# Zero fills of the edge matrix: eight small transfers for one, each tied to an earlier edge scatter

## The chip, the cores and the metric

The kernel runs on one core of a Trainium2 chip. The core has five engines, each with its own instruction queue: TensorE (PE), VectorE (DVE), ScalarE (ACT), GpSimd (POOL) and SyncE (SP), and sixteen DMA engines. The metric is the device time of one execution in microseconds (us). The time before is given as the median of five runs.

## What is computed

A network block of two layers over a graph with 3125 nodes and 50,000 edges (sorted by destination), 256 features. Each layer adds a graph convolution and an attention to the node features, and then a mixture of experts. Only the graph convolution of layer 0 matters here:

```python
def _L0_gnn_ref(input, edge_index, edge_weight, weight, bias):
    support = jnp.matmul(input, weight)
    row, col = (edge_index[0], edge_index[1])
    msgs = support[col] * edge_weight[:, None]
    output = jax.ops.segment_sum(msgs, row, num_segments=input.shape[0])
    return output + bias
...
xn = _layernorm(x, axis=-1)
x = x + _L0_gnn_ref(xn, edge_index, edge_weight, ...) + _L0_mix_ref(xn[None], ...)[0]
x = x + _L0_ffn_ref(_layernorm(x, axis=-1)[None], ...)[0]
```

## The kernel before

The convolution is done with a dense matrix of edge weights, `adj`, which lies in the chip's main memory (DRAM) and has 3200 x 3200 float32 elements. It goes through five steps.

1. *Zeros.* `adj` is cut into 25 pieces of 128 rows (`PIECE`, 1.6 MB). A DMA on SP's queue fills a piece from a tile of zeros (`fill`, L444 to L451, issued at L447). The tile has 128 x 800 elements and is read four times in one DMA, so the DMA has 512 rows of 3,200 bytes.
2. *Chunks.* The edges are cut into 16 chunks (`WIDTHS`: 8 and 12 columns, ten of 32, then 16, 16, 12 and 7; a column is 128 edges). SP loads a chunk's edges (`edge_load`, L372; the tiles of 32 columns have five buffers, so a load waits until DVE is done with the chunk five back). DVE works out the weights, with duplicate edges summed (`ch_code`, `ch_same`, `ch_prod`, `ch_sum`), and each edge's place in `adj` (`ch_place`, L415).
3. *Scatters.* POOL issues one indirect DMA per column (L75, `adj<-ch_sum,ch_place`, 391 in all), and behind each a small memset as a spacer (`spaced`, L286; the memset `idle`, L290). A chunk's scatters wait for the fills of all pieces that the chunk may touch ("zeros below").
4. *Row loads.* SP reads rows of `adj` back into SBUF (`load`, L541, two loads of 896 and 704 KB a piece), waiting for the scatters of the chunks that reach them.
5. *Runs.* PE multiplies them with the support (`sup`) in six runs of 4, 4, 4, 4, 4 and 3 pieces (`RUNS`, L572), DVE adds the results to `gT` (L578). Two last pieces come later.

Between these, PE, DVE and ACT sort the edges of the second layer in small steps (`sort_by_low`): DVE makes one-hot tiles (`s_hot`, L1350; `wi`, `we`, `wc`, L1353; `s_z`, L1361), ACT makes others (L1356, L1359), and PE multiplies them (L1377, L1382). `s_hot` has three buffers, so DVE waits for the matmul that read the one three steps back.

The order on PE, DVE, ACT and SP is the order of the program text. A generator `chunks()` is called on by estimated times (`advance`), and after each chunk's DVE work it puts that chunk's later edge load and some fills into SP's queue. Pieces that chunk c needs are numbered by `pieces_of(c)`: 1, 2, 4, 6, 8, ... 22, 23, 24, 25, 25. Before, the end of chunk c's work fills up to `pieces_of(c + 3)`; pieces 0 to 5 are filled by explicit calls ahead of it. Every hardware DMA, of SP and ACT alike, also carries one of eight semaphores and waits for the earlier DMA that had it.

Of the kernel before, what the change touches and what calls it, by code (L numbers as in the profile page):

```python
# [9 lines left out]
F32 = mybir.dt.float32  # L10
# [14 lines left out]
NP = NT * P  # L25
# [15 lines left out]
WIDTHS = (8, 12) + (32,) * 10 + (16, 16, 12, 7)  # L41
ENDS = [128 * sum(WIDTHS[:i]) for i in range(len(WIDTHS) + 1)]
EP, EW = 80, 625
PIECE = P * NP
# [5 lines left out]
PARTS = ((0, 4 * WIDE), (4 * WIDE, NP))  # L50
SW = 264
STEPS = 5
AHEAD = 90.0
RATE = 1.38

# [17 lines left out]
def scatter(nc, table, idx, rows, add=False):  # L73
    kw = {"compute_op": OP.add} if add else {}
    return nc.gpsimd.indirect_dma_start(  # L75
        out=table, out_offset=bass.IndirectOffsetOnAxis(ap=idx, axis=0),
        in_=rows, in_offset=None, **kw)


def pieces_of(c):  # L80

    return min(NT, (ENDS[c + 1] + DRIFT) // (16 * P) + 1)
# [35 lines left out]
def overlapping(ap, start, steps):  # L118

    return bass.AP(tensor=ap.tensor, offset=ap.offset + start,  # L120
                   ap=[list(ap.ap[0])] + [list(s) for s in steps])
# [6 lines left out]
class Kernel:  # L128
# [247 lines left out]
    def edge_chunk(self, pool, c):  # L376


        nc = self.nc
        e0 = ENDS[c]  # L380
        F, K = WIDTHS[c], HALO
        dst, src, W = self.chunk_in.pop(c)
        C = pool.tile([128, F + 2 * K], F32, name="ch_code", bufs=2)
        nc.vector.scalar_tensor_tensor(C, dst, float(NP), src, op0=OP.mult, op1=OP.add)
        same = pool.tile([128, F + K, K], BF16, name="ch_same", bufs=1)
        prod = pool.tile([128, F, K], F32, name="ch_prod", bufs=1)
        yield
        step = -(-F // 2) if F > 16 else F
        for f0 in range(-K, F, step):
            f1 = min(F, f0 + step)  # L390
            m = f1 - f0
            nc.vector.tensor_tensor(same[:, f0 + K:f1 + K, :], C[:, f0 + K:f1 + K, None].to_broadcast([128, m, K]),
                                    overlapping(C, f0 + K + 1, [[1, m], [1, K]]), OP.is_equal)
        yield
        for f0 in range(0, F, step):
            f1 = min(F, f0 + step)
            nc.vector.tensor_mul(prod[:, f0:f1, :], same[:, f0 + K:f1 + K, :],
                                 overlapping(W, f0 + 1, [[1, f1 - f0], [1, K]]))
        yield
        more = pool.tile([128, F], F32, name="ch_more", bufs=2)  # L400
        nc.vector.tensor_reduce(more, prod, AX.X, OP.add)
        wsum = pool.tile([128, F], F32, name=f"ch_sum{F}", bufs=4 if F == 32 else 2)
        nc.vector.tensor_add(wsum, more, W[:, :F])

        yield
        dup = pool.tile([128, F], F32, name="ch_dup", bufs=2)
        flat = same.rearrange("p i k -> p (i k)")
        nc.vector.tensor_reduce(dup, overlapping(flat, K - 1, [[K, F], [K - 1, K]]), AX.X, OP.max)
        own = C[:, K:K + F]
        off = pool.tile([128, F], F32, name="ch_off", bufs=2)  # L410
        nc.vector.scalar_tensor_tensor(off, self.number[F], float(BEHIND + e0), own,
                                       op0=OP.add, op1=OP.subtract)
        nc.vector.scalar_tensor_tensor(off, dup, self.off, off, op0=OP.max, op1=OP.mult)
        place = pool.tile([128, F], I32, name=f"ch_place{F}", bufs=4 if F == 32 else 2)
        nc.vector.tensor_add(place, off, own)  # L415
        ready = pieces_of(c)
        for f in range(F):
            ins = self.spaced(scatter(nc, self.adj[:], place[:, f:f + 1], wsum[:, f:f + 1]))
            for i in range(ready):
                self.after(ins, self.fills[i], "zeros below")  # L420
            self.tc.declare_no_dep(ins.ins, group="adj read", reason="blocks that are complete")
            for i in range(ready, NT):
                self.tc.declare_no_dep(ins.ins, group=f"zeros {i}", reason="rows behind the chunk's")
            for i in range(c + 1):
                self.tc.declare_no_dep(ins.ins, group=f"edges {i}", reason="places of their own")
            self.tc.add_to_no_dep_group(f"edges {c}", ins.ins)
            self.edge_scatters.setdefault(c, []).append(ins.ins)


    def layer0(self):  # L430
        nc, tc, a = self.nc, self.tc, self.a
        with ExitStack() as c:
# [5 lines left out]
            near = c.enter_context(ExitStack())  # L438
            ed = near.enter_context(tc.tile_pool(name="l0e", bufs=1))
            self.adj = self.dram.tile([BEHIND + 128 * NJ, 1], F32, name="adj")  # L440
            zero = ed.tile([128, NP // 4], F32, name="zero")
            nc.vector.memset(zero, 0.0)

            def fill(stop):  # L444
                for i in range(len(self.fills), stop):
                    rows = self.adj[i * PIECE:(i + 1) * PIECE].rearrange("(p r s) o -> p r (s o)", p=128, r=4)
                    ins = nc.sync.dma_start(rows, zero[:, None, :].to_broadcast([128, 4, NP // 4]))  # L447
                    for c in self.edge_scatters:
                        tc.declare_no_dep(ins.ins, group=f"edges {c}", reason="rows behind the chunk's")
                    tc.add_to_no_dep_group(f"zeros {i}", ins.ins)  # L450
                    self.fills.append(ins.ins.name)  # L451

            self.chunk_in, self.edge_scatters, self.fills, self.chunks_done = {}, {}, [], 0
            early = c.enter_context(ExitStack())
            big = early.enter_context(tc.tile_pool(name="l0x", bufs=1))
            order = self.edge_order(ed)
            next(order)
            self.edge_load(ed, 0, nc.sync)
            fill(1)
            for i in range(1, 3):  # L460
                self.edge_load(ed, i, nc.sync)
            self.load_x(nc.scalar)
            parts = [self.edges_by_tile(big), self.message_weights(big)]
            for g in parts:
                next(g)
            fill(4)
            for i in range(3, 7):
                self.edge_load(ed, i, nc.sync)
            fill(6)
            self.number = {}  # L470
            for F in sorted(set(WIDTHS)):
                self.number[F] = ed.tile([128, F], F32, name=f"number{F}")
# [2 lines left out]
            def chunks():  # L475
                for c in range(len(WIDTHS)):
                    steps = self.edge_chunk(ed, c)
                    for i in range(STEPS):
                        yield RATE * (ENDS[c] + (ENDS[c + 1] - ENDS[c]) * i / STEPS) / 128 - AHEAD
                        next(steps, None)  # L480
                    for _ in steps:
                        pass
                    self.chunks_done = c + 1
                    if c + 5 < len(WIDTHS) and c + 5 > 6:
                        self.edge_load(ed, c + 5, nc.sync)
                    fill(pieces_of(min(c + 3, len(WIDTHS) - 1)))
                yield 1e9

            prepared = chunks()
            due, now = next(prepared), 35.0  # L490

# [1964 lines left out]
```

## Time and profile before

| | |
|---|---|
| median of five runs | 3126.36 us (3106.69 to 3156.18) |
| profiled execution | 3102.36 us, span 3100.6 us |
| mean granted TensorE clock in it | 0.832 of full speed |
| PE busy | 2133.7 us (69%) |
| DVE busy | 1471.1 us (47%) |
| ACT busy | 823.6 us (27%) |
| POOL busy | 1699.5 us (55%) |
| fills of `adj` (L447) | 25, 1600 KB each |
| scatters into `adj` (L75) | 391, first at 22.1, last at 670.2 us |
| row loads of `adj` (L541) | 50, first at 335.6, last at 785.9 us |

All views of the profile come from one execution, taken by the hardware's profiler. "Busy" counts instructions at work and leaves out issues of DMAs; SP, which does nothing else, has no busy time. A wait is put down to the instruction whose semaphore came last ("releaser"); "issue" is time in which an engine waited for nothing that the profile shows, "remote" is a release that it can't assign. "PEld" is the loading of weights into TensorE and runs beside its matmuls. Lines (L75 and so on) are lines of the kernel before.

When the scatters of each chunk ran, in the profiled execution (us):

| chunk | start to end | chunk | start to end |
|---|---|---|---|
| 0 | 22.1 to 33.7 | 8 | 368.9 to 414.2 |
| 1 | 41.0 to 57.3 | 9 | 425.7 to 470.2 |
| 2 | 57.7 to 103.2 | 10 | 481.1 to 528.0 |
| 3 | 103.6 to 148.1 | 11 | 528.4 to 571.7 |
| 4 | 148.4 to 192.1 | 12 | 597.7 to 622.9 |
| 5 | 225.6 to 273.1 | 13 | 623.3 to 645.4 |
| 6 | 273.5 to 319.8 | 14 | 645.8 to 661.7 |
| 7 | 320.2 to 368.5 | 15 | 662.1 to 671.2 |

The matmuls of the six runs: 340.8 to 388.0, 387.8 to 448.3, 454.4 to 503.4, 590.7 to 643.2, 694.0 to 743.8 and 747.1 to 787.4 us. The fills left SP at 9.9 (piece 0), 34 to 40 (1 to 3), 52 to 86 (4 to 13), 210 (14, 15), 254 to 259 (16 to 19), 347 (20, 21), 390 (22) and 484 (23, 24); the row loads of runs 0 to 5 from 335.6, 367.9, 423, 484.8, 619 and 720 us.

### The profile page before, as it was taken

The numbers are of one execution on the slowest core, as the hardware profiler recorded it, in microseconds if no ns is written. First come the engines' busy times: TensorE is split into PE (matmuls) and PEld (weight loads), VectorE is DVE, ScalarE is ACT, GpSimd is POOL, SyncE is SP. The second block draws the span as 40 slices with busy tenths as digits, with TensorE's granted clock in tenths as the row PEclk, the third lists the DMA queues.
The fourth block names the chain that finished last, engine by engine and source line by source line (L and its number), as shares of the span: only waits on it lengthen the run. The fifth ranks groups of instructions, "written<-read, shape, count | busy, mean of one in ns | idle before, by whom it ended". The sixth has DMA issues, their size and how long they took to land.

```text
span 3100.6 us, 26794 instructions
## 1 busy us (share of the span) xinstructions
PE 2133.7 (69%) x8219; PEld 1479.8 (48%) x8219; DVE 1471.1 (47%) x3847; ACT 823.6 (27%) x1789; POOL 1699.5 (55%) x2187
## 2 busy tenths in 40 slices
PE   0555786569889998989984567676959222279944
PEld 0333353235455777777873344444646111146623
DVE  7348856565634941111114677777674000023345
ACT  0233143344422122222222233342014000012213
POOL 5858877550004446666630777778755888820011
PEclk9776797679859999999996798898978656689977
DMA  8312456022001245555533221222211001101122
GB/s 283 108 43 89 178 180 205 1 86 87 8 27 61 80 142 168 171 168 164 180 118 100 67 46 46 47 47 52 48 48 31 8 8 14 16 13 53 45 75 87
DMA packets 191718, 263.29 MB, mean 85 GB/s; under 512 B 57234, under 2 KB 152071, under 8 KB 191563
## 3 DMA queue, kind: packets, MB, share of 16 engines
q1 hardware_dynamic: 137551, 211.02, 20.6%
q0 software_dynamic: 48864, 45.64, 6.8%
q10 hardware_dynamic: 5148, 4.80, 0.5%
q8 instruction: 67, 1.10, 0.1%
q14 instruction: 88, 0.72, 0.1%
HBM read 180.80 MB, written 80.55 MB: 84 GB/s over the span
## 4 chain that ended last, share of the span: by engine, by line
PE 30%; issue 15%; DVE 11%; POOL 11%; another core or an unknown queue 9%; ACT 3%; DMA 2%; DVEq 0%; SPq 0%; POOLq 0%; ACTq 0%
POOL g L68 11%; PE pb L1137 6%; PE fpy L1867 5%; PE fph L1851 5%; PE pc L1146 4%; PE pb L572 3%; PE pb L615 1%; PE pc L1377 1%; DVE d_cum L1243 1%; PE pc L572 1%; PE fpy L2169 1%; DMA g<-tab,t_src 1%; DVE v L1623 1%; PE pb L273 1%
## 5 line engine op out<-in xcount | busy, mean ns | idle before, releaser
L68 POOL DMA_INDIRECT g<-tab,t_src x391 | 471.5, 1206 | 202.6 <-issue 199.3
L75 POOL DMA_INDIRECT adj<-ch_sum,ch_place x391 | 410.6, 1050 | 170.6 <-issue 63.8
L75 POOL DMA_INDIRECT sorted<-src,pos x256 | 245.2, 958 | 141.3 <-issue 77.9
L1851 PE MATMUL fph<-xT,fw 128*128 128x512 f32 (+2 forms) x448 | 193.4, 579 | 184.8 <-ACT fh L1853 172.0
L1137 PE MATMUL pb<-xs,w 128*128 128x256 f32 x1024 | 245.3, 395 | 44.8 <-ACT h L1139 41.5
L68 POOL DMA_INDIRECT G<-tabg,g_src x256 | 244.2, 954 | 42.7 <-issue 42.7
L1137 PEld LDWEIGHTS pb<-xs,w 128*128 128x128 f32 x1024 | 199.7, 197 | 85.3 <-ACT h L1139 49.9
L1629 PE MATMUL pw<-v,hot 128*128 128x260 f32 x782 | 231.1, 460 | 0.0
L1146 PE MATMUL pc<-w,h 128*128 128x256 f32 x1024 | 226.1, 379 | 0.0
L1851 PEld LDWEIGHTS fph<-xT,fw 128*128 128x128 f32 x448 | 89.8, 204 | 270.3 <-ACT fh L1853 178.1
L1867 PE MATMUL fpy<-fw,fh 128*128 128x256 f32 (+1 forms) x800 | 185.4, 390 | 34.5 <-issue 34.5
L572 PE MATMUL pb<-adj,sup 128*128 128x448 f32 (+1 forms) x484 | 199.1, 557 | 14.3 <-DVE r_tot L1248 13.6
L1146 PEld LDWEIGHTS pc<-w,h 128*128 128x128 f32 x1024 | 192.2, 190 | 24.9
L1139 ACT ACTIVATE h<-pb,b 128x256 f32<-128x256 f32 x256 | 115.8, 473 | 317.8 <-issue 248.3
L1853 ACT ACTIVATE fh<-fph,cols 128x512 f32<-128x512 f32 (+2 forms) x112 | 69.7, 632 | 487.7 <-remote 256.8
L1629 PEld LDWEIGHTS pw<-v,hot 128*128 128x128 f32 x782 | 177.0, 232 | 34.9
L1867 PEld LDWEIGHTS fpy<-fw,fh 128*128 128x128 f32 (+1 forms) x800 | 154.5, 194 | 70.3 <-issue 45.6
L68 POOL DMA_INDIRECT g_r<-sums,g_ati x25 | 24.5, 978 | 273.1 <-DMA sums<-g_joint 265.8
L1359 ACT ACTIVATE s_z<-s_y,s_val 128x128 f16<-128x128 f16 x256 | 112.4, 486 | 195.6 <-issue 190.7
L290 POOL MEMSET idle<- 128x128 f32 x697 | 154.2, 221 | 15.5 <-remote 12.5
L75 POOL DMA_INDIRECT slots<-rows,abi x50 | 58.1, 1163 | 164.6 <-DVE which L1060 154.9
L1869 DVE TENSOR_TENSOR acc<-fpy,fb 128x256 f32<-128x256 f32 (+1 forms) x25 | 10.6, 424 | 283.9 <-remote 217.3
(570 smaller groups left out, 3861.5 us busy)
## 6 DMA issues: line engine op xcount, KB each, us to landing
adj<-zero SPq DMA_DIRECT2D x25, 1600.0 KB
w<-in_L_ffn_W1p_dram SPq DMA_DIRECT2D x32, 1024.0 KB
w<-in_L_ffn_W2p_dram SPq DMA_DIRECT2D x32, 1024.0 KB
adj<-adj SPq DMA_DIRECT2D x24, 896.0 KB
adj<-adj SPq DMA_DIRECT2D x24, 704.0 KB
slots<-empty SPq DMA_DIRECT2D x1, 8448.0 KB
srow<-slots SPq DMA_DIRECT2D x32, 264.0 KB
adj<-ch_sum,ch_place POOLq DMA_INDIRECT x391
```

The costliest lines, as they stand in the source:

```text
L68: return nc.gpsimd.indirect_dma_start(out=out, out_offset=None, in_=table, in_offset=bass.IndirectOffsetOnAxis(ap=idx, axis=0))
L75: return nc.gpsimd.indirect_dma_start(out=table, out_offset=bass.IndirectOffsetOnAxis(ap=idx, axis=0), in_=rows, in_offset=None, **kw)
L290: rest = self.nc.gpsimd.memset(self.idle, 0.0)
L572: nc.tensor.matmul(pm[:, :w], sup[:, b, k * 128:(k + 1) * 128], mats[b, h][:, c0 - PARTS[h][0]:c0 - PARTS[h][0] + w], start=(b == b0), sto ...
L1137: nc.tensor.matmul(ph, w1[:, k, f * 128:(f + 1) * 128], xs[:, k, :], start=(k == 0), stop=(k == 1))
L1139: nc.scalar.activation(h[:, f, :], ph, AF.Gelu, bias=b1[:, f:f + 1])
L1146: nc.tensor.matmul(py, h[:, f, i * 128:(i + 1) * 128], w2[:, f, :], start=(f == 0), stop=(f == FC - 1))
L1359: nc.scalar.activation(z[:, i, k, :], y, AF.Relu, bias=val[:, k, s], scale=val[:, 2 + k, s])
L1629: nc.tensor.matmul(pw.rearrange("p h c -> p (h c)"), hot[:, k, :], v[:, k, :, :].rearrange("p h c -> p (h c)"), start=(k == 0), stop=(k == ...
L1851: nc.tensor.matmul(ph[:, :m], w1[:, k, f * 128:(f + 1) * 128], xT[:, k, t0 * P:t0 * P + m], start=(k == 0), stop=(k == 1))
L1853: nc.scalar.activation(hs[:, f, :m], ph[:, :m], AF.Gelu, bias=self.col("L1_ffn_b1", ei * FC + f))
L1867: nc.tensor.matmul(py[:p], hs[:, f, i * P:i * P + p], w2[:, f, :], start=(f == 0), stop=(f == FC - 1))
```

## The change

Each piece is filled by eight DMAs in place of one: the zero tile is 128 x 400 elements, and a small fill writes one of eight column blocks of the piece's 128 partition rows (128 rows of 1,600 bytes, 200 KB). There are 200 of them for 25. The early call for pieces 4 and 5 goes away; chunk 1's work issues them. The end of chunk c's work now fills up to `pieces_of(c + 2)` for `pieces_of(c + 3)`. And from chunk 2's on, the n-th small fill issued there waits for the spacer memset behind a scatter of chunk c - 2: the fills are spread evenly over that chunk's scatters (`edge_marks`). A scatter waits for all eight small fills of each piece below it. The order of instructions on PE, DVE, ACT and POOL stays as it was; SP has 175 more.

```diff
+SUBS = 8
...
             for i in range(ready):
-                self.after(ins, self.fills[i], "zeros below")
+                for name in self.fills[i]:
+                    self.after(ins, name, "zeros below")
...
             self.edge_scatters.setdefault(c, []).append(ins.ins)
+            self.edge_marks.setdefault(c, []).append(self.spacer)
...
-            zero = ed.tile([128, NP // 4], F32, name="zero")
+            zero = ed.tile([128, NP // SUBS], F32, name="zero")
             nc.vector.memset(zero, 0.0)
 
-            def fill(stop):
-                for i in range(len(self.fills), stop):
-                    rows = self.adj[i * PIECE:(i + 1) * PIECE].rearrange("(p r s) o -> p r (s o)", p=128, r=4)
-                    ins = nc.sync.dma_start(rows, zero[:, None, :].to_broadcast([128, 4, NP // 4]))
+            def fill(stop, beside=()):
+                todo = [(i, r) for i in range(len(self.fills), stop) for r in range(SUBS)]
+                for n, (i, r) in enumerate(todo):
+                    rows = self.adj[i * PIECE:(i + 1) * PIECE].rearrange("(p r s) o -> p r (s o)", p=128, r=SUBS)
+                    ins = nc.sync.dma_start(rows[:, r, :], zero)
+                    if beside:
+                        self.after(ins, beside[n * len(beside) // len(todo)], "beside the scatters")
                     for c in self.edge_scatters:
                         tc.declare_no_dep(ins.ins, group=f"edges {c}", reason="rows behind the chunk's")
                     tc.add_to_no_dep_group(f"zeros {i}", ins.ins)
-                    self.fills.append(ins.ins.name)
+                    if r == 0:
+                        self.fills.append([])
+                    self.fills[i].append(ins.ins.name)
...
             for i in range(3, 7):
                 self.edge_load(ed, i, nc.sync)
-            fill(6)
...
-                    fill(pieces_of(min(c + 3, len(WIDTHS) - 1)))
+                    fill(pieces_of(min(c + 2, len(WIDTHS) - 1)), self.edge_marks.get(c - 2, ()))
```

More of the change, by code (lines that the diff above doesn't have):

```diff
@@ L450, in fill @@
                     tc.add_to_no_dep_group(f"zeros {i}", ins.ins)
-                    self.fills.append(ins.ins.name)
+                    if r == 0:
+                        self.fills.append([])
+                    self.fills[i].append(ins.ins.name)
             self.chunk_in, self.edge_scatters, self.fills, self.chunks_done = {}, {}, [], 0
+            self.edge_marks = {}
             early = c.enter_context(ExitStack())
```

## The prediction

> **What bounds the kernel now.** I read four views in this order: the page's slices, a table of busy time per 100 us, the waits of the instructions that touch `adj`, and the waits and the chain of the stretch that the chain runs through. The edge matrix belongs to the first 790 us of 3100; nothing behind it is touched. First the page (share of busy time in tenths, 77.5 us a slice):
>
> ```profile
> span 3100.6 us, 26794 instructions
> ...
> PE   0555786569889998989984567676959222279944
> ...
> DVE  7348856565634941111114677777674000023345
> ...
> POOL 5858877550004446666630777778755888820011
> PEclk9776797679859999999996798898978656689977
> DMA  8312456022001245555533221222211001101122
> ```
>
> The first slice is full of transfers (DMA 8), the second and third nearly empty (3, 1), and there the clock and DVE fall too. The same in stretches of 100 us (busy us of PE, PEld, DVE, ACT, POOL, each with its count; granted clock; DMA share; GB/s):
>
> ```profile
> 0.00:100.00 100.00, 25.07 (x80) 16.33 (x80) 67.89 (x164) 13.59 (x26) 65.98 (x120) 0.98 0.89 299
> 100.00:200.00 100.00, 40.95 (x94) 23.67 (x95) 30.29 (x78) 22.38 (x40) 81.34 (x132) 0.62 0.03 5
> 400.00:500.00 100.00, 96.36 (x306) 53.12 (x306) 70.39 (x179) 42.03 (x92) 69.37 (x109) 0.98 0.63 211
> 500.00:600.00 100.00, 40.38 (x202) 20.36 (x200) 47.31 (x166) 32.79 (x85) 65.20 (x109) 0.59 0.12 43
> 600.00:700.00 100.00, 75.04 (x337) 38.16 (x334) 68.49 (x244) 44.33 (x114) 63.26 (x100) 0.83 0.20 67
> ```
>
> In 100 to 200 and in 500 to 600 POOL scatters, few bytes move (5 and 43 GB/s), and DVE and PE, which both have work, do half of what they do elsewhere. What POOL itself waits for:
>
> ```profile
> L447 SPq DMA_DIRECT2D adj<-zero x25: 513/637/4585, 9.9 to 484.1; - x25
> ...
>   DVE ch_place L415: 59.1, 2
>   DMA adj<-zero: 25.4, 2
> ```
>
> The fills are early everywhere but ahead of chunks 0 and 1 (18.3 + 7.1 us by the timeline). POOL loses more to late places (33.5 us ahead of chunk 5, 25.8 ahead of chunk 12), and these are late because DVE stalled. The waits of 490 to 690 us:
>
> ```profile
> ACT s_z L1359 <- issue: 127.1, 17, 19.4
> ...
> DVE s_hot L1350 <- remote: 50.2, 6, 19.9
> POOL adj L75 <- DVE ch_place L415: 25.8, 1, 25.8
> ```
>
> "remote" names no releaser. By the timeline each such stall of `s_hot` ends long after the PE matmul that frees its buffer (up to 13 us after), the last when chunk 11's scatters end at 571.7. I call this the crawl: PE's releases are seen late. It held in 105 to 182 (some 62 us of idle DVE), 514 to 572 (50 us) and 643 to 674 (25 us). Before 1000 us it appears only where POOL scatters without a break, PE and DVE have little queued, and little else moves; fills and row loads had ended at 100.5 and 508, just ahead of its first two onsets. With transfers running (40 to 50 us at some 300 GB/s, 375 to 405 at some 200) or with dense matmuls (225 to 345) it is absent. That is a correlation, and my forecast hangs on it. The chain of waits up to 800 us starts where the second crawl ends:
>
> ```profile
> 566.51 6.54 issue
> 573.05 2.02 PE pc L1377 x8
> ...
> 590.79 5.21 PE pb L572 x8
> ```
>
> From run 3's first matmul (590.8) on it is PE's work, broken by the crawl of 643 to 674.
>
> **The change part by part.**
>
> *Smaller fills.* 200 issues for 25. A fill's issue now takes 0.637 us (median); edge loads with as many rows as a small fill (128) take 0.33 to 0.46. SP gets 200 x 0.33 to 0.64 = 66 to 128 us for 25 x 0.64 = 16: +50 to +112 us, 23 to 52 of it in the first 100 us. SP computes nothing; what is queued there is edge loads and row loads. Packets become 1,600 bytes for 3,200. The trace has 139 ns for 3,200 bytes and 54 for 1,056; on the line between, 76 ns. So 12,800 x 139 / 16 = 111 us of the sixteen DMA engines become 25,600 x 76 / 16 = 122: +10 us spread over 500 us, and 4 to 5 in the saturated first 100.
>
> *First fills.* Each hardware transfer waits for an earlier one on one of eight semaphores, so at most 8 x 200 KB are under way; chunk 0 waits for all eight parts of piece 0. Its places are ready at 20.9 and its first scatter starts at 22.1, so a loss shows at once and a gain is at most 1 us. Chunk 1 started at 41.0, 7.1 us after it could. From -7 (the wait gone) to +6 (24 issues at the 1.3 us seen between 41 and 55 us, not 0.6, for pieces 1 to 3). ACT's input loads share the eight semaphores: 0 to +5. POOL idles 33.5 us ahead of chunk 5, which covers all this unless DVE slips too. I take 0, and 5 for the slow end.
>
> At this point the Trainium skill speaks against the change: "DMA: Bandwidth & Descriptors", Rules, asks for transfers of a MiB or more for 75% of the peak, and its fit (2.0 us + bytes / 436 GB/s, of software transfers) would by my estimate give 8 x 2.46 = 20 us for a piece in eight against 5.7 in one, one after the other. The row: at 60 to 90 us, with up to eight under way, fills and edge loads of some 50 KB together moved 350 GB/s, so I expect fixed parts to overlap. By the rule alone POOL would start chunk 1 some 14 us later; I don't take it.
>
> *The waits.* From piece 6 on the n-th small fill waits on the memset behind a scatter of chunk c-2 (152 of the 200). Behind a waiting fill on SP stand the next edge load and the next run's row loads, nothing else. Mostly the scatter has long passed when SP arrives, since SP is held earlier by edge loads that wait for free tiles (pieces 14, 15 left only at 210, 16 to 19 at 254 to 259). I find two real waits: pieces 10 and 11 beside chunk 2 (57.7 to 103.2; one per two scatters, 2.8 us; SP arrives near 84), and piece 24 beside chunk 10 (481.1 to 528.0; 1.47 us a scatter, one fill per four: 5.9 us, the last at about 523). Run 3's row loads, issued from 484.8 now, then leave from about 523 and land by about 541. Run 3 started at 590.7, so 50 us cover this, if the crawl stays; if run 3 could start earlier, these loads are next to be late.
>
> *Order.* PE, DVE, ACT and POOL keep their order; only SP's changes. The early fill of pieces 4 and 5 goes behind chunk 1's work, and two pieces fewer are filled by 100 us.
>
> *What traffic beside the scatters is worth.* Transfers in 508 to 541 (34 GB/s of fills, then 6.4 MB of rows at some 300) now lie in the second crawl. If traffic ends it, the twelve sort steps between run 2 and run 3 take their free pace: seven took 17.4 us in 573.0 to 590.4, so 12 x 2.5 = 30 us from 508 to 515 on, done by 545. Run 3 starts at about 543, 48 us earlier. Chunk 12's places are then ready when chunk 11 ends (572 for 597.7), so the scatters end near 645 for 671. But run 3 then ends at 595, and the next sort stretch (50.8 us now) lies beside scatters until 645 with only small traffic. If it crawls as 643 to 673 did, 20 to 24 us are left after 645: run 4 at 665 to 669, a gain of 25 to 29. If it doesn't crawl, run 4 starts at 630: 64. I take 30, nearest to the row that crawled.
>
> **The sum** on the profiled run: 3100.6 + 1.8 us around it = 3102.4; less 30 = 3072. The median of the five runs is 24 above the profiled one, so on it: 3126 - 30 = 3096.
>
> **The rivals.**
>
> *A, forecast (0.42):* 3096; own range 3062 (64 gained) to 3126 (run 3's held loads eat it).
>
> *B, no change (0.26):* traffic has nothing to do with the crawl; it lasts while POOL scatters, and run 3 starts at 590 with its loads long landed. Included: the change doesn't do what it says, since by my count all but about 15 of the 152 waits are over before SP arrives. Against it: the onsets at 100.5 and 508. 3126, with the spread of 16 either way that most of the five runs show.
>
> *C, slower (0.32):* the traffic that held off the first crawl shrinks. Two pieces fewer are filled before 100 us, and from 84 on the last seven parts come at one per 2.8 us (71 GB/s). If 71 GB/s isn't enough, the crawl starts 12 to 16 us earlier, and DVE and chunk 5's places slip by as much; with ACT's 0 to 5, the packets' 0 to 10 and chunk 1's 0 to 6 that is +12 to +37. It decides from 7 us on, the most that POOL can gain ahead of chunk 1. For it: chunk 5 already waits 33.5 us for its places, so any slip of DVE there is passed on. Against it: run 3 starts 19 us after the second crawl's end, behind sort steps, and could absorb some. 3138 to 3163, at 3148.
>
> On the pages' side of A and C: "SBUF — State Buffer", Who interferes with whom, says that a DMA never contends with a compute engine. That would leave only B; the rows say nothing of the reason, only of the times.
>
> **How the numbers follow.** About 1% (31 us) is what can be told from no change. Below 3095: 0.7 of A, 0.30. Above 3158: a quarter of C, 0.08, and as much as 0.12 more because C's price is read from a single stretch, and a crawl that starts early may cost more than its earlier start. The rest, 0.50, is within. The range 3060 to 3160 takes in A's two ends, B and two thirds of C.
>
> **What would show it.** Right: fills in the trace between 484 and 523 one per 5.9 us, run 3's loads from 523, the `s_hot` stalls of 514 to 572 gone or half, run 3 before 550, chunk 12 at 572. Wrong: those stalls unchanged beside the traffic (B); DVE's first long stall at 85 to 95 and chunk 5 after 230 (C); the wait of POOL on fills above 31 us, or ACT's first work well after 46, would mean that small fills are slower than I think; and if the fills' waits show from chunk 3 on, I have misjudged when SP arrives.

## The result, and the profile after

The changed kernel took 3152.6 us (median of 29 runs, 3121.2 to 3191.5), the kernel before 3126.4 us (median of 55): 26 us slower. The ratio is 1.0098 with a 95% interval of 1.0076 to 1.0120; like every ratio below it leaves out runs more than 1.5% above the fastest of their kernel, and the medians of all runs give 1.0084. The forecast was 30 us faster.

The page of the changed kernel's profiled execution, first the span and the slices (the same rows as before; a slice is 79 us now):

```profile
span 3164.8 us, 27158 instructions
...
DVE  7255956456733672111113477777665000023345
...
POOL 6848767660003316666650477787864888830011
PEclk9676698679959899999997688988878765689977
DMA  8212346222001125555543222212111101101122
```

DVE's digits of the second to fourth slice are 2, 5, 5 where they were 3, 4, 8: the low digits reach one slice further. The busy times by stretches of 100 us (PE, PEld, DVE, ACT, POOL, each with its count; clock; DMA share; GB/s):

```profile
0.00:100.00 100.00, 22.60 (x76) 14.95 (x76) 65.79 (x160) 13.00 (x25) 66.72 (x121) 0.98 0.79 250
100.00:200.00 100.00, 39.52 (x89) 21.29 (x90) 26.42 (x60) 19.48 (x36) 78.72 (x132) 0.63 0.08 21
400.00:500.00 100.00, 93.05 (x271) 51.90 (x270) 53.09 (x126) 42.54 (x88) 66.92 (x108) 0.96 0.60 207
500.00:600.00 100.00, 45.80 (x207) 23.52 (x205) 48.23 (x153) 23.40 (x60) 80.21 (x128) 0.67 0.44 144
600.00:700.00 100.00, 74.56 (x280) 35.16 (x280) 63.11 (x205) 34.42 (x89) 63.60 (x102) 0.79 0.14 49
```

The first row shows the small fills: 250 GB/s for 299 in the first 100 us. The fourth shows that the transfers did move beside the second crawl, 144 GB/s for 43, and that DVE did hardly more for it (48.2 us for 47.3). The waits of 490 to 690 us say the same of `s_hot` (the line was L1350):

```profile
DVE s_hot L1358 <- remote: 48.4, 4, 19.2
...
POOL adj L76 <- DVE ch_place L416: 22.1, 1, 22.1
```

It was 50.2 us in 6 stalls. By the timeline of DVE its second stall, 13.0 us from 551.2 to 564.2, lies wholly beside run 3's row loads, which moved 297 GB/s in these 13 us:

```profile
564.16 0.37 DVE L1358 TENSOR_TENSOR s_hot<-s_iota,s_high 128x200 bf16<-128x200 bf16 x1 [12.96 <-remote]
```

(start, length, engine, line, what, and in brackets the idle time before it). SP's queue there:

```profile
508.51 41.92 SPq L451 DMA_DIRECT2D adj<-zero  x24
550.52 19.24 SPq L549 DMA_DIRECT2D adj<-adj  x8
```

The last fills trickle for 42 us, and run 3's row loads leave behind them. So SP did what was forecast, some 25 us later, and the crawl went on.

Matched instruction by instruction, DVE's work is 6 us late at chunk 5's places (231.5 us for 225.6), 25 us late at 306, 29 at 814 and 61 at 1030, where POOL scatters again (`slots`, from 965 us in the first trace and 994 in this one). The two profiled executions are 64 us apart, the medians 26: the shown execution of before lies 24 us below its median, that of after 14 us above. So no difference between these two traces is evidence by itself, and the experiments were made for that reason.

### The profile page after: what moved, and what is told of

Read it like the earlier page. It is cut to its first block, busy times and chain, and to the rows that moved or that the text cites. A ratio compares the mean times of both kernels' runs of the same rounds, so it can differ in the third digit from the quotient of the medians.

```text
span 3164.8 us, 27158 instructions
## 1 busy us (share of the span) xinstructions
PE 2148.0 (68%) x8219; PEld 1482.5 (47%) x8219; DVE 1467.6 (46%) x3847; ACT 824.1 (26%) x1789; POOL 1687.2 (53%) x2187
## 4 chain that ended last, share of the span: by engine, by line
PE 40%; issue 16%; DVE 15%; another core or an unknown queue 12%; POOL 9%; ACT 4%; DMA 2%; SPq 0%; DVEq 0%; ACTq 0%; POOLq 0%
POOL g L69 8%; PE pb L1145 6%; PE fph L1859 6%; PE fpy L1875 5%; PE pb L580 5%; PE pc L1154 4%; PE pb L950 2%; PE pc L963 2%; PE pc L580 2%; PE pb L274 2%; PE pb L623 1%; DVE v L1631 1%; PE pw L1637 1%; DVE s_z L1369 1%
## 5 line engine op out<-in xcount | busy, mean ns | idle before, releaser
L76 POOL DMA_INDIRECT slots<-rows,abi x50 | 50.4, 1007 | 165.0 <-DVE which L1068 155.0
```

The source lines that it names most:

```text
L76: return nc.gpsimd.indirect_dma_start(out=table, out_offset=bass.IndirectOffsetOnAxis(ap=idx, axis=0), in_=rows, in_offset=None, **kw)
```

## The experiments

Each set of kernels ran on one chip, with runs of before beside them. Before itself took 3190, 3188, 3141, 2633 and 2634 us (medians) in the five sets. Whether the chips differ or only their state isn't known; I say "chip", and name each set by its time of before. The sets ran on chips that the record numbers 8, 8, 10, 1 and 10: the one at 3141 and the one at 2634, 22 minutes later, carry the same number. If that is one and the same chip, the speed belongs to a state that changes and not to the chip. The diffs show only the lines that matter.

### Parts of the change (before: 3190 us)

```diff
 e1_split: SUBS = 8, fills as before the change, no waits
-fill(pieces_of(min(c + 2, ...)), self.edge_marks.get(c - 2, ()))
+fill(pieces_of(min(c + 3, ...)))     and the early fill(6) again
 e2_order: whole fills (SUBS = 1, tile 128 x 800 read four times), c + 2, no waits
 e3_split_order: as changed, no waits
-fill(pieces_of(min(c + 2, ...)), self.edge_marks.get(c - 2, ()))
+fill(pieces_of(min(c + 2, ...)))
 e4_order_marks: as changed, whole fills
```

> Split alone: each fill is eight small DMAs, but they go out where they went out before (three chunks ahead, pieces 4 and 5 early) and wait for no scatter. Measured change of all parts together: 1.0098 (26 us of medians). Theory S, the small transfers themselves (175 more issues on SP, less moved per transfer, so that the inputs of DVE and PE come later): 1.008 to 1.011, and DVE 5 us or more behind at chunk 5's places (224.6 us before). Rival O, the later order of the fills: 0.998 to 1.002. Rival M, the waits on scatters: 0.998 to 1.002.

> Order alone: whole fills of 1.6 MB, two chunks ahead in place of three, no early fill of pieces 4 and 5, no waits on scatters. S: 0.998 to 1.002. O, the fills of pieces 14 to 19 fall later, into the stretch around 270 us in which DVE waited 18.7 us: 1.008 to 1.011. M: 0.998 to 1.002.

> Split and order together, without the waits on scatters. S: 1.008 to 1.011, as the split alone. O: 1.008 to 1.011, as the order alone. M: 0.998 to 1.002; then run 3's row loads leave some 40 us earlier, and the whole loss is the waits'.

> Order and waits, unsplit: whole fills of 1.6 MB, each waiting for one scatter of two chunks back. S: 0.998 to 1.002. O and M: 1.008 to 1.011 (e2 tells them apart). If no single kernel of the four is above 1.004, the loss is made by the parts together.

Measured: e1 1.0013 (0.9964 to 1.0062), e2 1.0032 (0.9990 to 1.0074), e3 1.0014 (0.9957 to 1.0071), e4 1.0012 (0.9965 to 1.0060). None is above 1.004. With a standard deviation of some 20 us from run to run, twelve runs can't tell 0.3% from nothing. Nor is it shown that there was a loss to divide: the changed kernel itself gave only 1.0021 here (f1, below).

### The changed kernel, a finer split, and the crawl's cause (before: 3188 us)

```diff
 f0_before, f1_after: unchanged
 f2_split32: as e1_split
-SUBS = 8
+SUBS = 32
 f3_memsets: before, chunks 2 to 4
-ins = self.spaced(scatter(nc, self.adj[:], place[:, f:f + 1], wsum[:, f:f + 1]))
+self.spaced(nc.gpsimd.memset(self.idle, 0.0))
+ins = self.spaced(nc.gpsimd.memset(self.idle, 0.0))
```

> The kernel before, unchanged, for a profile on the same chip as the others. If the profiled run shown first was an ordinary one, run 0's first matmul comes at 341 plus or minus 8 us; if it was a lucky one, at 355 to 375, as in the four kernels of the last call (360 to 375 in their profiles) and in the changed kernel (365.8).

> The changed kernel, unchanged, on the same chip as the parts. If the change is slower wherever it runs: 1.007 to 1.013. If its loss depends on the chip, or on how stalls happen to fall, 0.998 to 1.005, as the four part kernels gave (1.0012 to 1.0032).

> The split alone, four times as fine: 32 DMAs of 50 KB a piece, 800 for 25, in the order of before, without waits on scatters. Theory S (the small transfers cost): SP needs 800 x 0.35 to 0.65 us for them, so inputs and fills come late and the ratio is 1.015 to 1.04. Against S: 0.998 to 1.006.

> The kernel before with the 96 scatters of chunks 2 to 4 replaced by memsets of about the same time on POOL (four of 0.22 us a column); those edges are left out of the edge matrix. If the scatters' transfers make the crawl: DVE idle between 100 and 190 us falls from some 70 us to under 15, run 0 starts 15 to 60 us earlier, ratio 0.98 to 0.99. If a busy POOL makes it: idle time and ratio stay (0.997 to 1.003).

*f0.* Run 0 began at 359.9 us, and DVE's work stood 19 us behind the first profile of before at 312 us and 71 at 1127: most of what looked like the change's doing in the two first traces is there without the change.

*f1.* 1.0021 (0.9970 to 1.0071), lower than the first result's interval.

*f2.* 1.0176 (1.0113 to 1.0240). Here SP is late from the start: chunk 2 starts at 90.7 us (59.0 in f0), because 96 issues for pieces 1 to 3 stand ahead of the edge loads in SP's queue. At eight parts chunk 2 isn't late (56.8 to 59.2 us in all profiles). So this is a cost that the change does not have.

*f3.* 0.9682 (0.9588 to 0.9776), 100 us, more than was expected of either cause. The row of 100 to 200 us in f0 and in f3:

```profile
100.00:200.00 100.00, 37.19 (x82) 19.55 (x83) 24.08 (x57) 18.69 (x34) 79.61 (x134) 0.60 0.04 8
```

```profile
100.00:200.00 100.00, 64.95 (x229) 43.28 (x229) 81.80 (x178) 49.77 (x84) 81.77 (x285) 0.81 0.26 90
```

POOL is as busy in both (79.6 and 81.8 us). With memsets in place of the indirect transfers DVE does 82 us of work for 24, PE 229 matmuls for 82. So a POOL that is busy with memsets doesn't make the crawl; the scatters do. Whether it is their transfers or what POOL does to issue them, f3 doesn't tell, since both are gone in it. Nor do scatters make it at once: from 161 us on chunk 5 scatters in f3 too, and DVE still works 34 of the 38 us up to 199, before a stall of 20.7 us begins at 199.7.

### Transfers beside the scatters (before: 3141 us)

```diff
 h1_traffic: before, after chunk 4's fills
+for n, mark in enumerate(self.edge_marks[3] + self.edge_marks[4]):
+    rows = spare[n * PIECE // 4:(n + 1) * PIECE // 4].rearrange("(p s) o -> p (s o)", p=128)
+    self.after(nc.sync.dma_start(rows, zero), mark, "beside the scatters")
 h2_after as f1_after, h3_split as e1_split, h4_order_marks as e4_order_marks
```

> The kernel before with 64 more transfers: 400 KB of zeros each to a spare piece of main memory that nobody reads, one behind each scatter of chunks 3 and 4, so that some 290 GB/s move between 103 and 192 us, where 0 to 12 did. If transfers beside the scatters end the crawl (step A of the prediction): DVE's stalls over 3 us between 85 and 235 us, 72 and 88 us in the two profiles of before, fall under 25, run 0 starts 15 us or more earlier, ratio 0.985 to 0.995. If they have nothing to do with it: stalls 65 to 100 us, ratio 0.997 to 1.004. If they make it worse: stalls over 100 us, ratio over 1.004.

> The changed kernel again, for the question whether its loss depends on the chip: 1.0098 on the chip of the first result (before at 3126), 1.0021 (0.997 to 1.0071) on the second (before at 3188). On a chip with before near 3126: 1.007 to 1.013. On one near 3190: 0.999 to 1.006. If chips are not the cause, this gives 1.007 to 1.013 at either.

> The split alone again (1.0013 on the second chip). Theory S2: the small transfers cost 3 to 9 us at chunk 5's places (start of chunk 5: 236.7 to 242.5 us with them, 231.0 to 233.8 without, on the second chip) and this is all that the change costs; on a chip with before near 3126 the ratio is 1.005 to 1.011, near 3190 1.000 to 1.005. Rival: the split costs nothing anywhere, 0.998 to 1.002, and the loss is the order's or the waits'.

> Order and waits without the split again (1.0012 on the second chip). S2: no loss on any chip, 0.993 to 1.002, and between run 2's end and run 3's start 50 to 75 us in place of 83 to 89. Rival (order or waits cost): 1.006 to 1.012 where before is near 3126.

*h1.* 0.9970 (0.9901 to 1.0038). The row of 100 to 200 us:

```profile
100.00:200.00 100.00, 37.63 (x88) 20.47 (x86) 27.03 (x71) 23.14 (x41) 79.17 (x132) 0.68 0.73 265
```

265 GB/s in place of 5, and DVE works 27 us of 100, for 30 in the first profile of before and 24 in f0. Its stalls over 3 us between 85 and 235 us come to 82 us, and run 0 starts at 347.0 us (340.8 and 359.9). So transfers at this rate beside the scatters don't end the first crawl.

*h2, h3, h4.* The changed kernel had a median of 3152 us (six runs) beside before's 3141; the ratio worked out for it, 0.9889 (0.9806 to 0.9972), rests on too few runs to be used. The split 0.9999 (0.9947 to 1.0050), order and waits a median of 3138 us (six runs, no ratio). Again the times tell nothing apart. The trace of h4 does as was expected of it in one point: run 3 starts 50.6 us after run 2's end (55.7 in e4, 87.3 and 87.4 in the two profiles of before). In h4 chunk 11 scatters from 524 to 577 us, and in 520 to 570 at most 3 GB/s move, as in the second crawl of before's first profile; yet DVE works 48.8 of these 50 us (6.3 there). So in one execution the second crawl stayed away with nothing moving beside it. The gain didn't last in either: in e4 run 4 starts at 725.4 us (728.5 in f0, on a chip of the same time), and in h4 63 us after run 3's end (50.8 in before's first profile).

### A full path, and a chip without the crawl (before: 2633 us)

```diff
 i1_full, j2_full: before, after chunk 4's fills
+def copies(first, count):
+    for n in range(first, first + count):
+        rows = spare[n * PIECE // 4:(n + 1) * PIECE // 4].rearrange("(p s) o -> p (s o)", p=128)
+        nc.sync.dma_start(rows, zero)
...
+if c == 4:
+    copies(0, 78)
 i3_full_both, j3_full_both: as these, behind run 3's row loads
+if b0 == 12:
+    copies(78, 60)
 i2_ahead1: before
-            fill(6)
-fill(pieces_of(min(c + 3, len(WIDTHS) - 1)))
+fill(pieces_of(min(c + 1, len(WIDTHS) - 1)))
```

> The kernel before with 78 more transfers of 400 KB to spare memory in SP's queue behind the fills of 90 us, waiting for no scatter: the transfers that end at 100 us before now run on without a gap, at some 350 GB/s, to about 185 us. Theory C2 (a fully busy transfer path holds the crawl off, 290 GB/s with gaps does not; so the small fills, 240 to 305 GB/s, let it start at 88 in place of 105): DVE's stalls over 3 us in 85 to 235 us fall from 72 to 88 under 35, run 0 starts 15 us or more earlier than in the profiles of before (341 and 360), ratio 0.985 to 0.995. Rival D (transfers have no part in it, the small fills cost in another way): stalls 65 to 100 us, ratio 0.998 to 1.004.

> The kernel before with whole fills one chunk ahead in place of three and no early fill: ten pieces by then in place of fourteen, so that the transfers end near 80 us and not at 100. C2: the crawl sets in at 82 to 92 us, the 17th matmul of the support (102.3 and 107.5 us in the two profiles of before, 103.9 to 129.3 with small fills) starts after 112, chunk 5 starts 5 us later on the same chip, ratio 1.002 to 1.010. D: 17th matmul before 110, ratio 0.998 to 1.002.

> As i1_full, and 60 more such transfers behind run 3's row loads, from about 505 to 575 us, beside the second crawl. C2: stalls of s_hot between run 2's end and run 3's start fall from some 50 to 60 us to under 20, run 3 starts 50 to 65 us after run 2's end in place of 83 to 89, ratio 0.97 to 0.988. D: 83 to 89 us between the runs, ratio 0.998 to 1.006 (the added transfers move 55 MB beside nothing that waits for them).

Measured: 1.0009 (1.0000 to 1.0018), 0.9994 (0.9985 to 1.0003), 1.0007 (0.9998 to 1.0016). These don't try C2, since on this chip there is no crawl to hold off. All runs of before lie within 11 us. The profile of i2_ahead1, scattering into the same matrix:

```profile
span 2632.9 us, 26795 instructions
...
100.00:200.00 100.00, 64.93 (x227) 43.10 (x227) 82.43 (x179) 49.80 (x84) 88.12 (x140) 0.81 0.27 89
```

DVE does 82.4 us, as in f3 without those scatters, while POOL scatters through the whole stretch. No release of PE is seen late. Run 3 starts at 459.6 us (590.7 in the first profile of before). The two spans differ by 468 us.

### The changed kernel without the crawl (before: 2634 us)

> The changed kernel, unchanged. On a chip like the last one (before at 2633 us, no release of PE seen late): if the change costs only through the stalls, 0.998 to 1.002; if the small transfers cost work of their own on the path, 1.003 to 1.010. On a chip with before at 3120 to 3190: 1.000 to 1.010, as in the three runs so far.

> The 78 added transfers from 90 to 185 us, as in i1_full, which met a chip without the stalls (1.0009) and so didn't try theory C2. On a chip with before at 3120 to 3190: C2 (a fully busy transfer path holds the stall off): DVE's stalls over 3 us in 85 to 235 us under 35 us, ratio 0.985 to 0.995; D: stalls 65 to 100 us, ratio 0.998 to 1.004. On a chip without the stalls: 1.000 to 1.002 by both, nothing told apart.

> The added transfers beside both stretches, as in i3_full_both. On a chip with before at 3120 to 3190: C2: run 3 starts 50 to 65 us after run 2's end, ratio 0.97 to 0.988; D: 83 to 89 us, 0.998 to 1.006. On a chip without the stalls: 1.000 to 1.002 by both.

The added transfers cost 1.0012 (1.0002 to 1.0022) and 1.0006 (0.9995 to 1.0018). The changed kernel: 1.0095 (1.0076 to 1.0114), 2656.0 us for 2633.5. That lies in the range set down for small transfers' own work on the path, but the trace shows another cause. Matched with i2_ahead1 (0.9994, level with before), DVE is level (0.5 us ahead) up to 455 us, 19.5 us behind at 470, 21 at 486, and stays so to 770. SP's queue in the changed kernel, and then in j2_full (fills and order of before):

```profile
408.90 0.43 SPq L364 DMA_DIRECT2D ch_edge_weight<-last_edge_weight  x1
409.44 61.26 SPq L451 DMA_DIRECT2D adj<-zero  x24
470.79 4.50 SPq L549 DMA_DIRECT2D adj<-adj  x8
```

```profile
408.64 0.43 SPq L363 DMA_DIRECT2D ch_edge_weight<-last_edge_weight  x1
409.12 1.21 SPq L447 DMA_DIRECT2D adj<-zero  x2
410.79 20.81 SPq L550 DMA_DIRECT2D adj<-adj  x8
```

SP arrives at the same time, 409 us. Where before needs 1.2 us for the last fills, the changed kernel needs 61.3, and run 3's row loads start at 470.8 for 410.8. SP's own waits of 400 to 480 us name the reason, and the timeline of PE the one who pays (the wait is in brackets):

```profile
SPq L451 <- POOL idle L291: 50.6, 14, 8.3
```

```profile
475.64 1.86 PE L580 MATMUL pb<-adj,sup 128*128 128x448 f32 x2 [16.51 <-DMA adj<-adj]
```

and in j2_full, where PE doesn't wait:

```profile
458.59 5.31 PE L581 MATMUL pb<-adj,sup 128*128 128x448 f32 x8
```

50.6 us in 14 waits for spacer memsets (`idle`, behind scatters of chunks 9 and 10), and PE's first matmul of run 3 starts at 475.6 after 16.5 us of waiting for its rows; in j2_full it starts at 458.6. The other 10.7 of the 61.3 us are the 24 issues. In j2_full the last of these row loads left at 431.6 us, 27 us ahead of run 3, so by my estimate the issues alone would have been covered, and the waits were not. Run 3 takes 56.1 us for 52.5, so another 4 are lost inside it. The last piece is needed by chunk 14, whose scatters start at 571.5 us here: its fills had 100 us in hand, and what stood behind them in the queue had none.

## Why the prediction was wrong, point by point

*Smaller fills:* right. The issue took 0.430 us in the median (0.33 to 0.64 forecast), a packet 75 ns (76), the fills 120 us of the sixteen engines (122). In 60 to 90 us 280 to 290 GB/s moved for some 350, yet chunk 2 started at 57.7 us as before. On the chip without the crawl DVE lost nothing up to 455 us.

*First fills:* right. Chunk 0 started at 21.1 us (22.1), chunk 1 at 40.5 (41.0). The 14 us that the Trainium skill's fit ("DMA: Bandwidth & Descriptors", Anatomy of one DMA) would by the prediction's estimate have added for chunk 1, with parts taken one after the other, did not come.

*The waits and who stands behind them:* right in place, wrong in worth. The two real waits are where I put them (95 to 112 us for pieces 10 and 11; the last fills from 508 to 550 in the first trace), and run 3's loads were named as next to be late. I covered them with 50 us that exist only while the crawl does. In the trace of after, with the crawl, the loads had left by 570 and run 3 began at 614.3: still covered, as in f1 (575 and 608.7) and h2 (549 and 600.0). On the chip without it the cover is gone, and by the trace they cost 21 of the 22.5 us.

*What traffic beside the scatters is worth:* this step failed. It took the crawl's onsets just behind 100.5 and 508 us, where transfers ended, for cause and effect, and put 30 us of gain on it. The transfers came as planned, and the gain didn't: `s_hot` stalled for 48.4 us in place of 50.2, 13 of them beside 297 GB/s, and run 3 began at 614.3 us in place of the 543 forecast, 86 us after run 2's end (87 before). h1 moved 265 GB/s beside the first crawl, and it stayed; in h4 the second stayed away with nothing moving. By f3 it is the scatters that the crawl needs, and by the chip at 2633 they alone are not enough. That both onsets lie where PE and DVE have little queued is a guess that no run here tried. A small misreading, on which no term hangs: 40 to 50 us moved 360 GB/s, not some 300.

*The rivals:* the result lies inside the stated range (3060 to 3160) only because that took in C, and in C's bounds (3138 to 3163). C's signs appear too: stalls over 3 us from 87.4 us on, chunk 5 at 231.5. But before had one at 90.0 as well, and the traffic that C argued from didn't hold the crawl off in h1. That C's number came out is luck as far as these runs show. What can be said for its other half, that DVE is later at chunk 5 with small fills (start of chunk 5, us, by chip):

| before at | whole fills | small fills |
|---|---|---|
| 3126 | 225.6 | 231.5 (changed) |
| 3188 to 3190 | 233.8 (f0), 231.7 (e2), 231.0 (e4) | 242.5 (e1), 236.7 (e3), 236.9 (f1) |
| 3141 | 226.3 (h1, with added transfers), 206.4 (h4) | 231.0 (h3), 230.2 (h2) |
| 2633 to 2634 | 196.1 (i1), 195.2 (i2), 194.2 (i3), 194.8 (j2), 196.6 (j3) | 193.6 (j1) |

On every chip with the crawl each small-fill profile is later than each with whole fills, by 3 us at the least; without it they are level. So small fills seem to lengthen the first crawl, mostly by 3 to 10 us. This is a pattern of single profiles; the times of the split alone (1.0013, 0.9999) don't show it.

*B* (no change) was right that transfers beside the scatters don't end the crawl; its time, 3126 with 16 either way, was too low by 10 us.

**What stays open.** The loss of 22.5 us where there is no crawl is read from the trace: SP's waits, the loads behind them, PE's wait. No kernel took only that wait away, and the version that it suggests, piece 24 filled without waits or behind run 3's loads, was not tried. Where the crawl is, the first result's 26 us are not settled: in the three traces the held loads are covered, the longer first crawl may account for a few us, and the repeats there (1.0021 with an interval of 0.9970 to 1.0071) are too wide. Executions in which the second crawl is short would lose their cover as well; no trace of the changed kernel shows one. Nor is it known whether a fully busy path (C2) holds the crawl off.

## What to carry to other kernels

A wait put on a transfer is a wait of everything behind it in that queue: before adding one, list the next entries and when each is needed with the stalls of the present profile taken out, since cover that consists of a stall is not cover. Two things that begin together in one trace (transfers end, stall begins) are a guess until one of them is moved alone; here one kernel with added transfers (h1) was enough to put it in doubt. And a profiled execution is one draw: run the kernel before again, beside the experiment, before reading a difference between two traces.

## What was not expected of the hardware

The same kernel took 2633 and 2634 us in two sets (27 and 23 runs, each within 12 us) and 3126 to 3190 in the others (runs spread over 65 to 80 us). What the traces show beside it is how late PE's releases reach the others while POOL scatters: up to 14 us in the first 700 us of before's first profile, up to 20 in f1 and 33 beside the `slots` scatters in the changed kernel's, none in the quick sets, with the same scatters at the same pace (chunk 3 took 44.5 us in before's first trace, 45.3 in i2). What makes it do the one or the other no run here shows; one chip number stands for both.
